# First attention: every third mask of the last two groups made by ScalarE and GpSimd, and the check of counts moved to the GraphSAGE rounds

## The chip, the core and the metric

The kernel runs on one core of a Trainium2 chip. A core has five engines that run their own instruction streams and wait for one another through semaphores: TensorE (PE in the profile, with its weight loads as PEld), VectorE (DVE), ScalarE (ACT), GpSimd (POOL) and SyncE (SP, which only starts transfers here). They share the on-chip memory SBUF; products of TensorE land in the smaller memory PSUM. The metric is the device time of one execution in microseconds (us); lower is better.

## The reference, cut to what matters

A graph of 3,125 nodes with 128 features and 100,000 edges goes through four layers, each with a residual:

```python
h = relu(layernorm(x));  x = x + gat(gat(h))            # two attention layers, 4 heads of 32
h = relu(layernorm(x));  x = x + lanczos(h, edge_weight)  # three products with the weighted graph
h = relu(layernorm(x));  x = x + graphsage(h)             # three rounds: h@Ws + mean over neighbours @Wn, norm, PReLU
h = relu(layernorm(x));  x = x + message_layer(h, edge_type_16)
```

One attention layer, for each head:

```python
e = leaky_relu(al_src[src] + al_dst[dst], 0.2)
w = exp(e - segment_max(e, dst)[dst])
out = segment_sum(h[src] * w / segment_sum(w, dst)[dst], dst) + b ;  x = relu(out)
```

The change touches two places of this: the sums over edges of the first of the two attention layers, and a test that the kernel makes on its own data.

## The kernel before, in words

**The graph as a matrix.** Nodes are laid out in NB = 25 blocks of P = 128. The kernel builds, on the chip, a dense matrix `counts` in 8-bit floats: `counts[source, destination]` is the number of edges between two nodes. It stays in SBUF from the build until the GraphSAGE layer ends. A matrix of summed edge weights goes to DRAM (`weights`) for the second layer.

`place_edges` first scatters the edge records into a table in DRAM, sorted by block of destination and block of source, with 782 indirect transfers that GpSimd issues (L1096). Then `build_block` is called for each of the 25 destination blocks: SyncE loads the slots of the block as soon as the scatters it needs have landed, TensorE transposes them into `keys`, VectorE makes one-hot matrices from the keys (`oh_s`, `oh_d` at L1190, `oh_w` at L1192), TensorE multiplies them into a PSUM bank (L1204, L1207), and ScalarE copies the bank to `counts` (L1211, a cast to 8 bits) and to `w_out` (L1212), whose transfer to DRAM it issues itself (L1215). For the first six blocks ScalarE also copies records into `rowed` (L1177) and keys into `wide_dl` (L1181) for the last layer.

**The check of counts.** The kernel checks that no entry of `counts` exceeds MOST = 15. At the end of each block L1217 runs one activation over the block's column of `counts` (128 x 3200 elements): Relu(counts - 15), written to `junk`, which nobody reads, and summed into one column of `above`. After the last group `above` is summed into a column of `bad` (L1451). `bad` is read by `is_general` (L1955), whose flag decides at the end of the program whether a slow general version has to run; for these inputs it doesn't.

**Attention by thresholds.** exp of a leaky ReLU takes one of two forms, by the sign of its argument, so the sum over edges of one head is split into two matrix products: one with all of `counts` (`u`, L1347), and one with the counts of those pairs whose source score plus destination score is positive. For the second, `attend` makes a mask for each head i and source block sb: a tile `over` of 128 sources by n x 128 destinations (n is the number of destination blocks in the group), bf16, that holds `counts` where `row > minus` and zero elsewhere. `row` is the destinations' scores, which TensorE transposes into PSUM (`ps_row`) once a head; `minus` is one score for each partition. VectorE makes such a mask in one instruction (L1365). TensorE multiplies it with `parts`, the features split in three bf16 terms (L1379), into PSUM tiles `ps_acc`; after the 25 source blocks of a head VectorE sums the three terms (`sums`, L1386), after having made the first two masks of the next head. Masks are made two source blocks ahead of TensorE. At the end of a group some small instructions finish the nodes (L1393 to L1406).

**Groups.** In the first attention the destinations are taken in seven groups: blocks 5 to 8, 9 to 12, 13 to 16, 17 to 20, 21 to 24, then 0 to 2 and 3 to 4. Each group's blocks are built just before it attends, so build and attention interleave. Here VectorE makes every mask: the tuple `pools` has `None` for `beside`, and the pool `stream` of `over` tiles has four buffers.

The second attention works on five groups of five blocks and already shares the masks: `beside` is a pair of pools, `row_of` also copies the row from PSUM into SBUF with ScalarE (L1483), and for every third source block (sb % 3 == 2, eight of 25) ScalarE makes Sign (L1359) and Relu (L1360) of row plus score into `above0` (two buffers), and GpSimd multiplies it by `counts` into `over` of its own pool (three buffers, L1362). Its `stream` has eight buffers. Between the attentions, `project_nodes` (its copies are `gat_xT`, L1268, and `sd`, L1274), `attention_factors` and `source_parts` prepare scores and features.

**The GraphSAGE layer** (`layer2`). For each of five groups of five blocks the input is normalised and `prepare(g, 0)` runs: TensorE transposes the nodes, ScalarE copies them out (`yT`, L1659), TensorE multiplies by the weights into one of two `ps_w` buffers (L1665; in the first round also L1672 for the skips), ScalarE copies `z` (L1667) and half of the skips, VectorE adds `own` (L1668), and `split3` splits z into three bf16 terms with casts on ScalarE and subtractions on GpSimd. Then three rounds: for each of 25 blocks TensorE multiplies `counts` by the terms (`ps_agg`, L1722), VectorE sums and scales; after each group `finish` normalises. After rounds 0 and 1 `prepare` runs for the next one. After round 1 `message_weights` loads the weights of the last layer (its `embT` is cleared at L1768).

**What sets the order.** Each engine runs its instructions in one order, fixed when the program is built. The building framework doesn't keep strictly to the order in which the code issues them: an instruction whose operands and memory are ready may be put ahead of ones that come earlier in the code. Memory is given out from pools that are opened and closed with the blocks of code; a tile in a pool that reuses memory has to wait for the last access to what lay there.

Of the kernel before, what the change touches and what calls it, by code (L numbers as in the profile page):

```python
# [7 lines left out]
F32 = mybir.dt.float32  # L8
BF16 = mybir.dt.bfloat16
I32 = mybir.dt.int32  # L10
U8 = mybir.dt.uint8
FP8 = mybir.dt.float8e4
# [888 lines left out]
class FastGnn(Gnn):  # L901
# [233 lines left out]
    def open_build(self, s, counts):  # L1135
        nc, tc = self.nc, self.tc
        self.counts = counts.tile([P, NB, NP], FP8, name="counts8")
        self.weights = self.dram.tile([NB, P, NP], F32, name="weights")
        self.wide = self.dram.tile([2, sum(N_SLOTS[:WIDE]) * P], BF16, name="wide")
        one = self.b_one = s.enter_context(tc.tile_pool(name="build", bufs=1))  # L1140
        self.b_slots = s.enter_context(tc.tile_pool(name="build_s", bufs=1))
        self.b_hot = s.enter_context(tc.tile_pool(name="build_hot", bufs=2))
        self.b_out = s.enter_context(tc.tile_pool(name="build_out", bufs=3))
        self.b_ps = s.enter_context(tc.tile_pool(name="build_ps", bufs=2, space=PSUM))
        self.b_keys = s.enter_context(tc.tile_pool(name="build_keys", bufs=1, space=PSUM))
        self.lane16 = one.tile([P, P, 2], BF16, name="lane16")
        nc.vector.tensor_copy(self.lane16, bc(self.lane[:, :, None], [P, P, 2]))
        self.minus_most = one.tile([P, 1], F32, name="minus_most")
        nc.vector.memset(self.minus_most, -MOST)
        self.above = one.tile([P, NB], F32, name="above")  # L1150
        self.junk = one.tile([P, NB, P], FP8, name="junk")

    def build_block(self, db):
# [28 lines left out]
        for x0 in range(0, n_slots, BATCH):  # L1182
# [10 lines left out]
            for x in range(k):  # L1193
# [15 lines left out]
                if last and (j == 1 or sb == NB - 1):  # L1209
# [3 lines left out]
                    if sb % 4 == 3 or sb == NB - 1:  # L1213
# [3 lines left out]
        nc.scalar.activation(self.junk, self.counts[:, :, db * P : (db + 1) * P], AF.Relu, bias=self.minus_most,  # L1217
                             accum_out=self.above[:, db : db + 1], saturate=False)
# [115 lines left out]
    def attend(self, suffix, a, b, pools):  # L1334
# [4 lines left out]
        n = b - a  # L1339
        at, cols = slice(a, b), slice(a * P, b * P)  # L1340
# [3 lines left out]
        for q in range(n):  # L1344
            wide = u_tile()
            for sb in range(NB):
                nc.tensor.matmul(wide[:, : HEADS * 3 * F1], lhsT=self.counts[:, sb, (a + q) * P : (a + q + 1) * P],  # L1347
                                 rhs=parts[:, sb, :, :, F1:], start=(sb == 0), stop=(sb == NB - 1))
            V.tensor_reduce(u[:, q], wide[:, : HEADS * 3 * F1].rearrange("p (h s f) -> p h f s", h=HEADS, s=3),
                            axis=AX.X, op=OP.add)  # L1350
        sums = None
        for i in range(HEADS):
            row, own = row_of(lambda j: bc(self.sd[:, a + j, 1, i : i + 1], [P, P]), n)

            def mask(sb, row=row, own=own, i=i):

                if beside and sb % 3 == 2:
                    above = beside[0].tile([P, most * P], BF16, name="above0")[:, : n * P]
                    nc.scalar.activation(above, own, AF.Sign, bias=self.sd[:, sb, 0, i : i + 1])  # L1359
                    nc.scalar.activation(above, above, AF.Relu)  # L1360
                    over = beside[1].tile([P, most * P], BF16, name="over")
# [46 lines left out]
    def graph_and_layer0(self, counts, node):  # L1408
# [3 lines left out]
        with ExitStack() as s:  # L1412
# [17 lines left out]
            with ExitStack() as s2:  # L1430
# [14 lines left out]
                with ExitStack() as s3:  # L1445
                    self.open_build(s3, counts)
                    for a, b in GROUPS:
                        for db in range(a, b):
                            self.build_block(db)
                        self.attend(1, a, b, pools)  # L1450
                    nc.vector.tensor_reduce(self.bad[:, 1:2], self.above, axis=AX.X, op=OP.add)  # L1451
# [175 lines left out]
    def layer2(self):  # L1627
        nc, tc = self.nc, self.tc
        last = 3 * D
        with ExitStack() as s:  # L1630
# [79 lines left out]
            for g in range(GN):  # L1710
# [3 lines left out]
                prepare(g, 0)  # L1714
            for i in range(3):
                n = last + (i == 0)
                ready = []
                for g in range(GN):
                    for db in range(g * GB, (g + 1) * GB):
# [10 lines left out]
                        nc.vector.scalar_tensor_tensor(own[:, db, :], t, inv, own[:, db, :], op0=OP.mult, op1=OP.add)  # L1730
                    finish(g, i)
# [3 lines left out]
                if i == 1:  # L1735
                    self.message_weights(one, ps_msg)
# [298 lines left out]
```

## Time and profile before

| what | value |
|---|---|
| median of 3 runs | 3201.25 us (3200.83 to 3203.47) |
| the profiled execution | 3195.56 us |
| its span | 3193.8 us, 52,069 instructions |
| granted TensorE clock, mean | 0.959 |
| PE busy | 2561.2 us (80%) |
| PEld busy | 1825.5 us (57%) |
| DVE busy | 2296.6 us (72%) |
| ACT busy | 917.4 us (29%) |
| POOL busy | 1445.2 us (45%) |

The stages, by the times at which their instructions run: scatter and build from the start, with the scatter's last issue at about 1,120 us; the first attention interleaved with the build until 1,300 us, its last two groups attending from 1,146 and from 1,258 us; projections until 1,343 us, when the second attention starts; the second layer from about 1,725 to 2,203 us; GraphSAGE from there until about 2,640 us; the message layer to the end.

How to read the lines. In the row of slices each digit is the busy share of an engine in one of 40 equal parts of the span, in tenths, 9 being 90% or more. A row of a group gives line, engine, operation, the tile written, "<-", the tiles read, the shapes (partitions x elements) and xcount, then after the bar the busy time in us and the mean of one in ns, and after the second bar the engine's idle time just before such instructions and who ended it. A row of a timeline gives start and duration in us (a run of equal instructions is joined, with its count), engine, line, operation and tiles, and in brackets the wait before it in us and its releaser. Neighbours overlap by some hundredths of a us to a tenth, so a cost per instruction is best read from start to start.

### The profile page before, as it was taken

How to read it: one execution, taken by the hardware profiler on the slowest of the kernel's cores; microseconds unless marked ns; L12 is line 12 of the kernel's file. 1: busy time of each engine (PE TensorE's matmuls, PEld its weight loads, DVE VectorE, ACT ScalarE, POOL GpSimd, SP SyncE). 2: the span in 40 equal slices, each digit the busy share in tenths (PEclk: the TensorE clock that was granted, in tenths of full speed). 3: DMA queues.
4: the chain of work that ended last, by engine and by line, in shares of the span. 5: the costliest groups of instructions: out<-in, count | busy, mean ns of one | idle time of the engine just before them, and what ended most of it. 6: DMA issues, size and time to landing. Idle time of an engine off the chain costs nothing. (4 is left out here: it accounts for less than half of the span.)

```text
span 3193.8 us, 52069 instructions
## 1 busy us (share of the span) xinstructions
PE 2561.2 (80%) x20788; PEld 1825.5 (57%) x20788; DVE 2296.6 (72%) x4015; ACT 917.4 (29%) x1785; POOL 1445.2 (45%) x1394
## 2 busy tenths in 40 slices
PE   0018787878787788798886999997999976989898
PEld 0017464646455655477675444445555546888897
DVE  7979999999989899899997010405455575666766
ACT  3035050505140212476665000002120212333333
POOL 1577777777777700055553000000120106777775
PEclk9979999999999999899999999998999997999999
DMA  6013130303131101000002878781000004444443
GB/s 187 14 18 98 25 98 20 98 20 101 31 94 28 51 32 62 1 2 1 1 1 80 298 272 302 273 301 45 1 1 1 5 18 138 130 139 133 128 131 85
DMA packets 127742, 276.54 MB, mean 87 GB/s; under 512 B 28645, under 2 KB 68468, under 8 KB 116532
## 3 DMA queue, kind: packets, MB, share of 16 engines
q1 hardware_dynamic: 62982, 198.30, 18.9%
q0 software_dynamic: 37856, 32.76, 4.8%
q10 hardware_dynamic: 26652, 42.05, 3.7%
q8 instruction: 165, 2.70, 0.4%
q14 instruction: 87, 0.71, 0.1%
HBM read 210.00 MB, written 63.02 MB: 85 GB/s over the span
## 5 line engine op out<-in xcount | busy, mean ns | idle before, releaser
L1096 POOL DMA_INDIRECT table<-rec,idx x782 | 773.6, 989 | 336.7 <-issue 237.4
L1365 DVE SCALAR_TENSOR_TENSOR over<-ps_row,minus,counts 128x512 bf16<-128x512 f32 (+3 forms) x1040 | 699.3, 748 | 15.9 <-ACT row L1483 12.0
L1379 PE MATMUL ps_acc<-parts,over 128*128 128x198 bf16 x5000 | 571.4, 251 | 134.1 <-POOL over L1362 34.7
L1379 PEld LDWEIGHTS <-over 128*128 128x128 bf16 x5000 | 391.8, 98 | 309.7 <-DVE over L1365 231.9
L1910 POOL DMA_INDIRECT m_far<-pre,src x401 | 397.8, 992 | 259.1 <-DVE skips L923 137.2
L1207 PE MATMUL ps_cw<-oh_w,oh_d 128*128 128x128 bf16 x4050 | 385.9, 224 | 56.7 <-DVE oh_w L1192 52.1
L1533 PE MATMUL ps_sum<-g,node 128*128 128x512 f32 (+1 forms) x1050 | 413.2, 552 | 12.9 <-DMA g<-weights 12.9
L1362 POOL TENSOR_TENSOR over<-above,counts 128x640 bf16<-128x640 bf16 x160 | 211.3, 1329 | 392.0 <-ACT above L1360 265.2
L1207 PEld LDWEIGHTS <-oh_d 128*128 128x128 bf16 x4050 | 303.8, 100 | 90.9 <-issue 68.7
L1204 PE MATMUL ps_cw<-oh_d,oh_s 128*128 128x128 bf16 x1350 | 299.0, 224 | 48.2 <-ACT w_out L1212 24.7
L1722 PE MATMUL ps_agg<-l_parts,counts 128*128 128x384 bf16 (+1 forms) x1875 | 317.3, 327 | 14.0 <-POOL l_parts L923 14.0
L1192 DVE TENSOR_TENSOR oh_w<-oh_s,keys 128x1024 bf16<-128x1024 bf16 (+2 forms) x561 | 325.4, 633 | 0.0
L1533 PEld LDWEIGHTS ps_sum<-g,node 128*128 128x128 f32 x1050 | 189.8, 192 | 222.1 <-issue 208.4
L1722 PEld LDWEIGHTS <-counts 128*128 128x128 fp8e4 x1875 | 183.5, 98 | 134.5 <-issue 11.3
L1754 POOL IOTA of_i<- 96x1 int32 x1 | 0.1, 135 | 480.2 <-PE ps_sum L1609 480.2
L1211 ACT ACTIVATE counts<-ps_cw 128x256 fp8e4<-128x256 f32 (+1 forms) x325 | 122.7, 378 | 303.9 <-PE ps_cw L1207 294.4
L1931 PE MATMUL agg_far<-m_far,oh_far 128*128 128x128 f32 x1246 | 173.8, 287 | 11.6 <-ACT m_far L1917 7.1
L1892 PE MATMUL agg_wide<-m_wide,oh_wide 128*128 128x128 f32 x1100 | 160.3, 289 | 26.5 <-ACT m_wide L1889 17.9
L1204 PEld LDWEIGHTS <-oh_s 128*128 128x128 bf16 x1350 | 133.6, 100 | 80.9 <-issue 49.9
L1347 PEld LDWEIGHTS <-counts 128*128 128x128 fp8e4 x1250 | 112.1, 98 | 102.3 <-ACT counts L1211 19.9
L1885 PE MATMUL ps_m<-skips,src_hot 128*128 128x128 bf16 x1650 | 159.3, 224 | 9.1 <-DVE src_hot L1875 9.1
L1931 PEld LDWEIGHTS agg_far<-m_far,oh_far 128*128 128x128 f32 x1246 | 156.6, 199 | 13.6 <-ACT m_far L1917 9.0
(353 smaller groups left out, 3532.1 us busy)
## 6 DMA issues: line engine op xcount, KB each, us to landing
g<-weights SPq DMA_DIRECT2D x75, 1024.0 KB
g<-weights SPq DMA_DIRECT2D x75, 576.0 KB
weights<-w_out ACTq DMA_DIRECT2D x150, 256.0 KB
src_row<-wide SPq DMA_DIRECT2D x32, 512.0 KB
table<-rec,idx POOLq DMA_INDIRECT x782
type_row<-wide SPq DMA_DIRECT2D x32, 384.0 KB
table<-none SPq DMA_DIRECT2D x1, 10864.0 KB
type_row<-types SPq DMA_DIRECT2D x25, 384.0 KB
```

The source lines that it names most:

```text
L1096: st = nc.gpsimd.indirect_dma_start(out=self.table, out_offset=bass.IndirectOffsetOnAxis(ap=idx[k][:, p : p + 1], axis=0), in_=rec[:, (k * ...
L1192: nc.vector.tensor_tensor(oh_w[:, t, :h], oh_s[:, :h], key(WT + t), op=OP.mult)
L1204: nc.tensor.matmul(ps[:, 0, j, :], lhsT=oh_s[of], rhs=oh_d[of], start=(j == c == 0), stop=last, skip_group_check=True)
L1207: nc.tensor.matmul(ps[:, 1, j, :], lhsT=oh_d[of], rhs=oh_w[:, t][of], start=False, stop=(last and t == 2), skip_group_check=True)
L1362: nc.gpsimd.tensor_tensor(over[:, : n * P], above, self.counts[:, sb, cols], op=OP.mult)
L1365: V.scalar_tensor_tensor(over[:, : n * P], row, minus[:, sb, i : i + 1], self.counts[:, sb, cols], op0=OP.is_gt, op1=OP.mult)
L1379: nc.tensor.matmul(banks[j // 2][:, j % 2, : 3 * F2], lhsT=over[:, j * P : (j + 1) * P], rhs=parts[:, sb, i].rearrange("p s f -> p (s f)") ...
L1533: nc.tensor.matmul(ps[:, c0 // 512, :m], lhsT=node[:, b, :], rhs=g[:, c0 - lo : c0 - lo + m], start=(b == 0), stop=(b == NB - 1))
L1722: nc.tensor.matmul(ps[:, :n], lhsT=self.counts[:, sb, db * P : (db + 1) * P], rhs=parts[:, sb, :n], start=(sb == 0), stop=(sb == NB - 1))
L1892: nc.tensor.matmul(agg, lhsT=oh[:, j, :], rhs=m[:, j, :], start=(x == 0), stop=(x == n_slots - 1))
L1910: nc.gpsimd.indirect_dma_start(out=m[:, j, :], out_offset=None, in_=pre, in_offset=bass.IndirectOffsetOnAxis(ap=src_of[:, a + j : a + j + ...
L1931: nc.tensor.matmul(agg[d], lhsT=oh[:, c - lo, :], rhs=m[:, c - a, :], start=(c == LOW[d]), stop=(c == ENDS[d] - 1))
```

## The change

Three things:

1. The tiles `minus_most`, `above` and `junk` leave the build's pool, and with them the memset, the 25 checks at the ends of the blocks, and the reduction after the last group.
2. In the first attention, groups 0 to 2 and 3 to 4 (`b <= FIRST`, FIRST = 5) use `shared` instead of `pools`: the row is also copied into SBUF by ScalarE (`two_rows`), and every third mask goes over ScalarE and GpSimd as in the second attention, with tiles 3 x 128 columns wide, two `above0` and three `over` buffers. `stream` keeps its four. The other five groups are as before. (`wide` is renamed `ps` where it named a PSUM tile.)
3. In `layer2`, before the rounds, the three tiles and the memset appear, and after the sums of a block in groups 1, 2 and 3 one check is issued as long as any is left: 15 in round 0 and ten in round 1. After round 1, before `message_weights`, `above` is summed into `bad`.

```diff
@@ -1145,10 +1145,6 @@
         self.b_keys = s.enter_context(tc.tile_pool(name="build_keys", bufs=1, space=PSUM))
         self.lane16 = one.tile([P, P, 2], BF16, name="lane16")
         nc.vector.tensor_copy(self.lane16, bc(self.lane[:, :, None], [P, P, 2]))
-        self.minus_most = one.tile([P, 1], F32, name="minus_most")
-        nc.vector.memset(self.minus_most, -MOST)
-        self.above = one.tile([P, NB], F32, name="above")
-        self.junk = one.tile([P, NB, P], FP8, name="junk")
 
     def build_block(self, db):
         nc, tc = self.nc, self.tc
@@ -1214,8 +1210,6 @@
                         b = sb // 4 * 4
                         nc.scalar.dma_start(self.weights[db, :, b * P : (sb + 1) * P].rearrange("p (b s) -> p b s", s=P),
                                             w_out[:, : sb + 1 - b])
-        nc.scalar.activation(self.junk, self.counts[:, :, db * P : (db + 1) * P], AF.Relu, bias=self.minus_most,
-                             accum_out=self.above[:, db : db + 1], saturate=False)
 
     def load_graph(self, dst, b, weights=False):
         self.nc.sync.dma_start(dst.rearrange("p b s -> p (b s)"), self.weights[b])
@@ -1337,16 +1331,17 @@
         V = nc.vector
         stream, done, u_tile, acc_tile, row_of, most, beside = pools
         n = b - a
+        wide = GW if most == GB else 3 * P
         at, cols = slice(a, b), slice(a * P, b * P)
         parts, minus = self.parts, self.gat_small[3]
         u = done.tile([P, most, HEADS, F1], F32, name="u")[:, :n]
         acc = done.tile([P, most, HEADS, F2], F32, name="acc")[:, :n]
         for q in range(n):
-            wide = u_tile()
+            ps = u_tile()
             for sb in range(NB):
-                nc.tensor.matmul(wide[:, : HEADS * 3 * F1], lhsT=self.counts[:, sb, (a + q) * P : (a + q + 1) * P],
+                nc.tensor.matmul(ps[:, : HEADS * 3 * F1], lhsT=self.counts[:, sb, (a + q) * P : (a + q + 1) * P],
                                  rhs=parts[:, sb, :, :, F1:], start=(sb == 0), stop=(sb == NB - 1))
-            V.tensor_reduce(u[:, q], wide[:, : HEADS * 3 * F1].rearrange("p (h s f) -> p h f s", h=HEADS, s=3),
+            V.tensor_reduce(u[:, q], ps[:, : HEADS * 3 * F1].rearrange("p (h s f) -> p h f s", h=HEADS, s=3),
                             axis=AX.X, op=OP.add)
         sums = None
         for i in range(HEADS):
@@ -1355,10 +1350,10 @@
             def mask(sb, row=row, own=own, i=i):
 
                 if beside and sb % 3 == 2:
-                    above = beside[0].tile([P, most * P], BF16, name="above0")[:, : n * P]
+                    above = beside[0].tile([P, wide], BF16, name="above0")[:, : n * P]
                     nc.scalar.activation(above, own, AF.Sign, bias=self.sd[:, sb, 0, i : i + 1])
                     nc.scalar.activation(above, above, AF.Relu)
-                    over = beside[1].tile([P, most * P], BF16, name="over")
+                    over = beside[1].tile([P, wide], BF16, name="over")
                     nc.gpsimd.tensor_tensor(over[:, : n * P], above, self.counts[:, sb, cols], op=OP.mult)
                 else:
                     over = stream.tile([P, most * P], BF16, name="over")
@@ -1444,11 +1439,21 @@
                          lambda: ps_acc.tile([P, 2, 256], F32, name="ps_acc"), row_of, 4, None)
                 with ExitStack() as s3:
                     self.open_build(s3, counts)
+                    rows = s3.enter_context(tc.tile_pool(name="gat_d", bufs=1))
+                    beside = [s3.enter_context(tc.tile_pool(name=f"gat_b{n}", bufs=n)) for n in (2, 3)]
+
+                    def two_rows(term, n):
+                        own = rows.tile([P, 3 * P], F32, name="row")[:, : n * P]
+                        whole, _ = row_of(term, n)
+                        nc.scalar.copy(own, whole)
+                        return whole, own
+
+
+                    shared = pools[:4] + (two_rows, 4, beside)
                     for a, b in GROUPS:
                         for db in range(a, b):
                             self.build_block(db)
-                        self.attend(1, a, b, pools)
-                    nc.vector.tensor_reduce(self.bad[:, 1:2], self.above, axis=AX.X, op=OP.add)
+                        self.attend(1, a, b, shared if b <= FIRST else pools)
                 with ExitStack() as s3:
                     tmp = s3.enter_context(tc.tile_pool(name="gat_h", bufs=1))
                     two = s3.enter_context(tc.tile_pool(name="gat_r", bufs=2))
@@ -1712,6 +1717,12 @@
                 self.normal(tmp, y[:, at], self.x[:, at], GB)
                 nc.vector.tensor_scalar(y[:, at], y[:, at], 0.0, None, op0=OP.max)
                 prepare(g, 0)
+
+            minus_most = one.tile([P, 1], F32, name="minus_most")
+            nc.vector.memset(minus_most, -MOST)
+            above = one.tile([P, NB], F32, name="above")
+            junk = one.tile([P, NB, P], FP8, name="junk")
+            unseen = list(range(NB))
             for i in range(3):
                 n = last + (i == 0)
                 ready = []
@@ -1728,11 +1739,16 @@
                         t = tmp.tile([P, D], F32, name="agg_t")
                         nc.vector.tensor_reduce(t, ps[:, :last].rearrange("p (s f) -> p f s", s=3), axis=AX.X, op=OP.add)
                         nc.vector.scalar_tensor_tensor(own[:, db, :], t, inv, own[:, db, :], op0=OP.mult, op1=OP.add)
+                        if unseen and 0 < g < GN - 1:
+                            b = unseen.pop()
+                            nc.scalar.activation(junk, self.counts[:, :, b * P : (b + 1) * P], AF.Relu, bias=minus_most,
+                                                 accum_out=above[:, b : b + 1], saturate=False)
                     finish(g, i)
                 if i < 2:
                     for g in range(GN):
                         prepare(g, i + 1)
                 if i == 1:
+                    nc.vector.tensor_reduce(self.bad[:, 1:2], above, axis=AX.X, op=OP.add)
                     self.message_weights(one, ps_msg)
```

## The prediction

> **What bounds the kernel now.** I read the page's slices first, then groups by line and shape, then timelines of single engines. The page's chain of waits covers only 46% of the span, roughly from 1,700 us on (its pieces after 2,203 us are used below), so the first attention is read from groups and timelines. The slices:
>
> ```profile
> DVE  7979999999989899899997010405455575666766
> ACT  3035050505140212476665000002120212333333
> POOL 1577777777777700055553000000120106777775
> ```
>
> A slice is 80 us. VectorE (DVE) is full in slices 3 to 16, build and both attentions. GpSimd (POOL) is idle in slices 14 to 16, where the last two groups attend (from 1,146 and 1,258 us), and ScalarE (ACT) is nearly idle there. The groups by shape between 1,100 and 1,330 us, and VectorE's timeline:
>
> ```profile
> L1365 DVE SCALAR_TENSOR_TENSOR over<-ps_row,minus,counts 128x384 bf16<-128x384 f32 x100 | 53.0, 622 | 0.0
> L1365 DVE SCALAR_TENSOR_TENSOR over<-ps_row,minus,counts 128x256 bf16<-128x256 f32 x100 | 39.6, 474 | 0.0
> ...
> 1161.61 13.22 DVE L1365 SCALAR_TENSOR_TENSOR over<-ps_row,minus,counts 128x384 bf16<-128x384 f32 x25
> 1174.73 0.84 DVE L1386 TENSOR_REDUCE acc<-ps_acc 128x132 f32<-128x396 f32 x2
> ...
> 1270.68 9.88 DVE L1365 SCALAR_TENSOR_TENSOR over<-ps_row,minus,counts 128x256 bf16<-128x256 f32 x25
> ```
>
> One head of group (0,3) is 25 masks and two sums, 13.87 us from 1,161.61 to the next head's 1,175.48; of (3,5), 10.27 us. VectorE never waits in them: it sets their time. A mask costs 0.53 us start to start at 384 columns and 0.39 at 256.
>
> **The change, part by part.** The sum is made against the profiled execution: 3,195.56 us, of which 3,193.8 are span. The shown median is 5.69 us above it, so I take the same difference off the median.
>
> *1. The check leaves the build.* 25 activations over 128x3200 go. ScalarE's timeline at one of them, and who waits:
>
> ```profile
> 1112.26 2.97 ACT L1217 ACTIVATE junk<-counts,minus_most 128x3200 fp8e4<-128x3200 fp8e4 x1
> ...
> 1115.22 0.22 ACT L1181 COPY wide_dl<-keys 128x76 bf16<-128x76 bf16 x1
> ...
> 1115.47 0.69 DVE L1190 TENSOR_TENSOR oh_s<-lane,keys 128x1024 bf16<-128x1024 bf16 x1 [2.24 <-ACT wide_dl L1181]
> ```
>
> A check holds ScalarE 2.96 us (1,112.26 to 1,115.22). Behind it waits the copy of keys, and for that VectorE: 2.26, 2.24 and 1.88 us at blocks 1, 2 and 4, together 6.4, which go. In the one-slot blocks 20 to 23 TensorE waits for ScalarE's `w_out` after a check (1.01, 1.60 and 1.42 us) and is the later engine until the block ends, so VectorE's waits there shrink by about 4. Elsewhere VectorE covers the check and nothing is won. Value **-10**; ends -6 (only the direct waits) and -14 (also the 2.09 us at 1,126.62, where TensorE runs slow after standing idle).
>
> *2. Every third mask on ScalarE and GpSimd.* VectorE makes 17 of 25: a head needs 17 x 0.525 + 0.75 = 9.7 us at 384 columns and 17 x 0.392 + 0.48 = 7.1 at 256. The eight others each take Sign and Relu on ScalarE and one multiplication on GpSimd. None is in the trace at these widths; the nearest rows are the second attention's, at 640:
>
> ```profile
> L1362 POOL TENSOR_TENSOR over<-above,counts 128x640 bf16<-128x640 bf16 x160 | 211.3, 1329 | 392.0 <-ACT above L1360 265.2 <-PE ps_acc L1379 123.5 <-POOL over L1362 1.9
> ...
> 1439.87 10.38 DVE L1365 SCALAR_TENSOR_TENSOR over<-ps_row,minus,counts 128x640 bf16<-128x640 f32 x13
> ```
>
> GpSimd at 384: 0.80 us if all of 1,325 ns scales, 0.83 if 0.1 us is fixed as in its smallest fill (98 ns); I take 0.80, and 0.55 at 256. ScalarE's steps fall by 0.83 ns an element, 0.21 us per operation at 384 and 0.32 at 256. The trace shows two rhythms at 640. With two `above0` buffers ScalarE often waits for GpSimd: two masks then cost 4.23 us (1,439.06 to 1,443.29). In the other rhythm a mask costs 1.59 us (1,355.69 to 1,357.28). The first becomes 4.23 - 2 x 0.50 - 0.43 = 2.8 a pair, 11.2 a head, at 384, and 2.1 and 8.3 at 256; the second 1.16 a mask, 9.8 with the row copy, and 8.0. The second attention's inner heads average 14.9 us (row copies at 1,435.97 and 1,480.66, three heads), near VectorE's own 17 x 0.79 + 1.24 = 14.7, so I stay near the faster rhythm: 10.5 and 8.2. That saves 4 x (13.87 - 10.5) + 4 x (10.27 - 8.2) = 13.5 + 8.3 = 21.8. Off it: filling and draining the chain at each group's ends, and ScalarE's copy of the next block's `rowed`, queued among the signs and waiting for its load (2.86 us in ScalarE's timeline at 1,153.80). Value **-19**. Ends: -12 (slow rhythm throughout), -27 (VectorE alone binds).
>
> A rule speaks against this part. The Trainium skill (SBUF — State Buffer, section SBUF: two separate sides) says that GpSimd holds a port pair for a whole instruction, and that a VectorE operation with two SBUF inputs stands still meanwhile. The row first: the 13 masks above took 0.798 us each beside a working GpSimd, against 0.79 from the shape alone. A mask has one tensor in SBUF (`counts`) and its row in PSUM. By the rule's lock eight multiplications would hold VectorE 8 x 0.80 = 6.4 us a head, more than the 4.2 it saves: part 2 would cost some 9 us in (0,3). The lock is real in this trace, where both inputs are in SBUF (0.35 us becomes 1.63 beside a GpSimd addition):
>
> ```profile
> 2281.76 2.18 POOL L1704 TENSOR_TENSOR skips<-skips,l_own 128x640 f32<-128x640 f32 x1 [24.94 <-DVE inv_col L1727]
> ...
> 2282.46 1.63 DVE L1730 SCALAR_TENSOR_TENSOR l_own<-agg_t,inv_col,l_own 128x128 f32<-128x128 f32 x1
> ```
>
> For masks I go by their row. Dispatch of the scatter is over by then (POOL has no instruction after 1,120 us), so GpSimd's queue is empty.
>
> *3. The build's memory frees earlier.* ScalarE's `gat_xT` waits 37.0 us for the reduction of `above` at L1451. With `above` gone that memory ends with block 4 at 1,258 us, and groups 1 to 4 of the second projection can start under group (3,5); their copies into `sd` still wait for the last signs, which read it. Group 0 needs the attention's result at 1,305.8. Value **-2**, ends 0 and -4.
>
> *4. The check enters the GraphSAGE stage.* By its place in the code a check follows a block's aggregation in groups 1 to 3 of rounds 0 and 1. There ScalarE idles 18.3 us between normalisations and TensorE's 97 us of products cover 15 checks (44 us). But an engine's order is made by readiness, not by place. VectorE's timeline has
>
> ```profile
> 2205.52 0.14 DVE L1768 MEMSET embT<- 32x96 f32 x1
> ```
>
> which stands behind round 1 in the code and runs 280 us before that. A check needs only `counts` and a bias memset like this one. So I expect checks as soon as layer 2's memory exists (2,203.4 us), in each pause of ScalarE. The preparation from 2,205.7 to 2,256.9 us has such pauses and no cover: TensorE starts its 97 us only when it ends. ScalarE's timeline for one group:
>
> ```profile
> 2233.36 0.37 ACT L1667 COPY z<-ps_w 128x256 f32<-128x256 f32 x1
> 2233.62 0.38 ACT L484 COPY skips<-ps_w 128x256 f32<-128x256 f32 x1
> 2236.16 0.37 ACT L1667 COPY z<-ps_w 128x256 f32<-128x256 f32 x1 [2.16 <-PE ps_w L1665]
> 2237.03 0.37 ACT L484 COPY skips<-ps_w 128x256 f32<-128x256 f32 x1 [0.49 <-PE ps_w L1672]
> 2237.79 0.27 ACT L1667 COPY z<-ps_w 128x128 f32<-128x128 f32 x1 [0.38 <-PE ps_w L1665]
> ...
> 2240.91 0.36 ACT L1667 COPY z<-ps_w 128x256 f32<-128x256 f32 x1
> ```
>
> A group takes 7.55 us (2,233.36 to 2,240.91) and calls ScalarE in about three visits, one per turn of the two `ps_w` buffers, with 3.5 us of copies and casts. A check in the pause before each visit makes it 3 x 2.96 + 3.5 = 12.4 us, +4.85. Behind a check wait z, then TensorE for the buffer, then GpSimd's `l_parts`, then the first sums. Four groups: +19.4; the first, which starts amid the normalisations and takes six checks, +5.5 by the same steps. Together **+25** for some 18 checks; the other seven fall under round 0 at no cost. Ends: 0 (all in the rounds), and +49.5 if the preparation takes all 25: 25 x 2.96 = 74, less the 24.5 us of pauses in that timeline. The moved final reduction (0.17 us) is nothing.
>
> Sum: -10 - 19 - 2 + 25 = **-6**: 3,189.6 for the profiled execution, **3,195 us** against the median.
>
> **The rivals.**
> *The checks stay in the rounds.* Part 4 is 0: -31, 3,170 us. For it: ScalarE's free 18.3 us, and that a placement could be kept. Against: embT, and the sum over `bad` for the end of the program, which runs at 1,316.85.
> *Slower: the preparation takes all 25 checks.* Place: ScalarE's queue, 2,205 to 2,257 us. If z and skip of one turn are called on separate visits, there are more than 25 pauses (the timeline has 28), and part 4 costs 49.5: -31 + 49.5 = +18.5, 3,220 us. It decides from 31 us on, about 21 checks at 1.5 net. Against: after a stop of 2.96 us both buffers are ready together.
> *Third masks come late.* TensorE takes masks in order and VectorE has four buffers here, eight in the second attention. If every pair stops VectorE, (0,3) gives 4 x 1.5 and (3,5) nothing, so part 2 is -4 with its losses: +9, 3,210 us. For it: the 34.7 us that TensorE waits for GpSimd's masks in the second attention; against: its inner heads of 14.9.
>
> **Chances.** Main case 0.50, own range 3,184 to 3,206; checks in the rounds 0.17; all checks in the preparation 0.18; late masks 0.15. A change under 0.2% (6.4 us) counts as none here. The main case lies near that bound: 0.26 faster, 0.22 same, 0.02 slower. Rival one is all faster; two is slower (0.16) or same (0.02); three 0.02, 0.05 and 0.08. Faster 0.45, same 0.29, slower 0.26. The range leaves out the lower half of rival one and most of rival two's upper half: 3,168 to 3,218.
>
> **What would show it.** L1365's 384 and 256 shapes fall to 68 each, with heads of 10.5 and 8.2 us between row copies. No wait for `wide_dl` at blocks 1, 2 and 4. The start of TensorE's long run of `ps_agg` comes about 51 us after layer 2's first square now; after, 76, with checks between z copies. The prediction is wrong if checks stand in the rounds, if masks make VectorE wait, or if ScalarE loads tables between Sign and the copies into `counts`.

## The result and the profile after

The changed kernel takes **3207.03 us** (median; 3203.33 to 3213.55) against 3201.25 us before: ratio **1.0018** (95% interval 1.0012 to 1.0024), 5.8 us slower. The prediction said 3,195 us, 6 us faster. The time lies inside the stated range, but the kernel became slower where it was to become faster.

The profiled execution of the changed kernel took 3210.43 us (span 3208.5), that of before 3195.56. Of the 14.9 us between them some 9 are a difference of executions: the one before is 5.7 us under its median, the one after 3.4 over. So I compare stages, between marks that both traces have; "(0, 3)" is the group of destination blocks 0 to 2.

| stretch, us | before | after | difference |
|---|---|---|---|
| start to the end of group (17, 21) | 865.5 | 866.5 | +1.0 |
| to the end of group (21, 25) | 131.7 | 127.2 | -4.5 |
| to the first mask of (0, 3) | 149.0 | 150.2 | +1.2 |
| to the end of (0, 3) | 64.8 | 50.7 | -14.1 |
| to the first mask of (3, 5) | 47.3 | 44.9 | -2.4 |
| to the end of (3, 5) | 46.5 | 41.6 | -4.9 |
| to the second attention | 40.0 | 35.8 | -4.2 |
| **sum up to the second attention** | 1344.9 | 1317.0 | **-27.9** |
| second layer's last product to TensorE's long run of `ps_agg` | 53.8 | 86.6 | **+32.8** |

An "end" here is the start of the addition of the bias to that group (L1405 before, L1400 after). The "preparation" below is the last row: the stretch of the GraphSAGE layer from the second layer's last product until TensorE runs `ps_agg` without a break. The second attention takes 388.6 us in both, from its first mask to its last addition of the bias; the second layer's products, which nothing touches, took 428.2 us in the execution of before and 433.4 in that of after, and 431 to 435 in the kernels of the first experiments. In the slices, ScalarE fills up where the GraphSAGE layer starts (slice 27), and GpSimd and ScalarE work in slices 14 and 15:

```profile
DVE  7979999999989898999993010413455575566766
ACT  3043040404121155766662000007420212233333
POOL 1577777777777732455551000001120106777775
```

VectorE's timeline in the last two groups, (0, 3) and then (3, 5), after the change:

```profile
1157.84 9.00 DVE L1360 SCALAR_TENSOR_TENSOR over<-ps_row,minus,counts 128x384 bf16<-128x384 f32 x17
1166.76 0.83 DVE L1381 TENSOR_REDUCE acc<-ps_acc 128x132 f32<-128x396 f32 x2
1167.51 9.01 DVE L1360 SCALAR_TENSOR_TENSOR over<-ps_row,minus,counts 128x384 bf16<-128x384 f32 x17
...
1263.11 6.74 DVE L1360 SCALAR_TENSOR_TENSOR over<-ps_row,minus,counts 128x256 bf16<-128x256 f32 x17
1269.77 0.56 DVE L1381 TENSOR_REDUCE acc<-ps_acc 128x132 f32<-128x396 f32 x1
1270.25 5.96 DVE L1360 SCALAR_TENSOR_TENSOR over<-ps_row,minus,counts 128x256 bf16<-128x256 f32 x15
```

A head is 17 masks and the sums, 9.67 us (1157.84 to 1167.51) and 7.14 us (1263.11 to 1270.25), with no wait: VectorE's own time, the best end of what the prediction allowed. GpSimd's multiplications beside it, by shape:

```profile
L1357 POOL TENSOR_TENSOR over<-above,counts 128x384 bf16<-128x384 bf16 x32 | 27.7, 868 | 34.7 <-PE ps_acc L1374 21.5 <-ACT above L1355 5.9 <-ACT counts L1207 5.0
L1357 POOL TENSOR_TENSOR over<-above,counts 128x256 bf16<-128x256 bf16 x32 | 20.3, 640 | 71.9 <-ACT counts L1207 45.7 <-PE ps_acc L1374 20.3 <-ACT above L1355 5.1
```

GpSimd needs 868 and 640 ns (800 and 550 were estimated). Eight of them a head are 6.9 us of GpSimd's time, and VectorE's masks beside them stay at 0.53 us: no lock held them. The rule that the prediction set against this part is, in its own words, one of two inputs in SBUF; a mask has one there (`counts`) and its row in PSUM, so the rule did not reach it.

ScalarE's timeline in the preparation, for about one group:

```profile
2214.51 3.02 ACT L1744 ACTIVATE junk<-counts,minus_most 128x3200 fp8e4<-128x3200 fp8e4 x1
...
2217.85 0.37 ACT L1672 COPY z<-ps_w 128x256 f32<-128x256 f32 x1 [0.23 <-PE ps_w L1670]
2219.07 0.37 ACT L484 COPY skips<-ps_w 128x256 f32<-128x256 f32 x1 [0.85 <-PE ps_w L1677]
2219.34 2.96 ACT L1744 ACTIVATE junk<-counts,minus_most 128x3200 fp8e4<-128x3200 fp8e4 x1
...
2223.23 0.77 ACT L1664 COPY yT<-ps_t 128x512 f32<-128x512 f32 x2
2223.86 3.00 ACT L1744 ACTIVATE junk<-counts,minus_most 128x3200 fp8e4<-128x3200 fp8e4 x1
2226.82 0.75 ACT L922 CAST l_parts<-rest 128x640 bf16<-128x640 f32 x1
2227.44 0.40 ACT L1672 COPY z<-ps_w 128x256 f32<-128x256 f32 x1
```

The checks stand there, between the copies of z. The first begins at 2,184.98 us, and 21 of the 25 start before TensorE's long run does. ScalarE is busy for 81.4 of the 86.6 us, against 24.0 of 53.7 without checks.

### The profile page after: what moved, and what is told of

Its sections match the earlier page's. It is cut to its first block, busy times and chain, and to the rows that moved or that the text cites. A ratio compares the mean times of both kernels' runs of the same rounds, so it can differ in the third digit from the quotient of the medians.

```text
span 3208.5 us, 52208 instructions
## 1 busy us (share of the span) xinstructions
PE 2552.6 (80%) x20788; PEld 1840.4 (57%) x20788; DVE 2267.3 (71%) x3951; ACT 977.3 (30%) x1921; POOL 1495.7 (47%) x1458
## 5 line engine op out<-in xcount | busy, mean ns | idle before, releaser
L1360 DVE SCALAR_TENSOR_TENSOR over<-ps_row,minus,counts 128x512 bf16<-128x512 f32 (+3 forms) x976 | 670.0, 759 | 16.5 <-ACT row L1488 12.0
L1374 PE MATMUL ps_acc<-parts,over 128*128 128x198 bf16 x5000 | 549.7, 251 | 123.7 <-POOL over L1357 34.8
L1357 POOL TENSOR_TENSOR over<-above,counts 128x640 bf16<-128x640 bf16 (+2 forms) x224 | 259.3, 1165 | 314.4 <-PE ps_acc L1374 165.2
L1354 ACT ACTIVATE above<-row,sd 128x640 bf16<-128x640 f32 (+2 forms) x224 | 166.7, 747 | 60.7 <-POOL over L1357 57.6
L1200 PEld LDWEIGHTS <-oh_s 128*128 128x128 bf16 x1350 | 133.7, 100 | 71.0 <-issue 50.5
```

Source lines behind the costliest of these rows:

```text
L1200: nc.tensor.matmul(ps[:, 0, j, :], lhsT=oh_s[of], rhs=oh_d[of], start=(j == c == 0), stop=last, skip_group_check=True)
L1357: nc.gpsimd.tensor_tensor(over[:, : n * P], above, self.counts[:, sb, cols], op=OP.mult)
L1360: V.scalar_tensor_tensor(over[:, : n * P], row, minus[:, sb, i : i + 1], self.counts[:, sb, cols], op0=OP.is_gt, op1=OP.mult)
L1374: nc.tensor.matmul(banks[j // 2][:, j % 2, : 3 * F2], lhsT=over[:, j * P : (j + 1) * P], rhs=parts[:, sb, i].rearrange("p s f -> p (s f)") ...
```

## The experiments

The expectations name theories by letters. **A**: the loss is the price of the checks in the preparation, and only there. **R**: leaving the build gained little because the check had stood in a wait of ScalarE. **G**: early signs of the shared masks wait for GpSimd's scatter. **P** and **S** are two ways of pricing a check in a pause. The rivals are in the expectations. Where nothing else is said, the edits are made to the changed kernel.

Four of these kernels (`twelve`, `short`, `anch_rowed` and `anch_both`) ran on another chip, where the kernel before takes 4366.94 us and the second attention starts some 940 us later (why that chip is slower is not known). I use them by stages, and their ratios only against that chip's own time before.

### Checks held in the rounds

```diff
-            minus_most = one.tile([P, 1], F32, name="minus_most")
-            nc.vector.memset(minus_most, -MOST)
+            minus_most = one.tile([P, NB], F32, name="minus_most")
...
                             b = unseen.pop()
-                            nc.scalar.activation(junk, self.counts[:, :, b * P : (b + 1) * P], AF.Relu, bias=minus_most,
-                                                 accum_out=above[:, b : b + 1], saturate=False)
+                            nc.vector.tensor_scalar(minus_most[:, b : b + 1], t[:, :1], 0.0, -MOST, op0=OP.mult, op1=OP.add)
+                            nc.scalar.activation(junk, self.counts[:, :, b * P : (b + 1) * P], AF.Relu,
+                                                 bias=minus_most[:, b : b + 1], accum_out=above[:, b : b + 1], saturate=False)
```

> The changed kernel, but each check takes its bias (-15) from a column that VectorE writes out of the sums of the block just aggregated, so it cannot run before that block's products. Theory A (the checks cost what they cost only because they stand in the preparation, where ScalarE has no cover): the trace shows 15 checks in round 0 and 10 in round 1, the preparation is back at about 53 us, and the kernel is 28 us faster than before (the changed kernel's own gain up to the second attention), ratio 0.991. Theory B (a check costs wherever it stands in this layer, because the squares and PReLU steps of the next group wait behind it): each of 25 checks still costs about 1.3 us, the rounds grow by 33 us, ratio about 1.002 as for the changed kernel.

Measured: 3174.81 us, ratio **0.9909** (0.9893 to 0.9924). The groups by tile (duration least/median/most in ns, then first and last start) and TensorE's timeline of this kernel:

```profile
L1744 ACT ACTIVATE junk<-counts,minus_most x25: 2963/2964/2966, 2257.5 to 2422.8; 128x3200 fp8e4<-128x3200 fp8e4 x25
```

```profile
2237.53 97.33 PE L1732 MATMUL ps_agg<-l_parts,counts 128*128 128x385 bf16 x587 [1.70 <-POOL l_parts L923]
```

All 25 checks run, each as long as before, and start between 2,257 and 2,423 us, beside TensorE's products; the preparation is 53.7 us and the rounds did not grow (363.6 us from the long run's start to the last product of `ps_agg`, 364.0 before). The same 25 instructions cost 33 us in one place and nothing in the other: theory A.

### No check, neither change, and the move alone

`no_check` drops the check from `layer2` (and with it the tiles and the memset):

```diff
-                        if unseen and 0 < g < GN - 1:
-                            b = unseen.pop()
-                            nc.scalar.activation(junk, self.counts[:, :, b * P : (b + 1) * P], AF.Relu, bias=minus_most,
-                                                 accum_out=above[:, b : b + 1], saturate=False)
...
-                    nc.vector.tensor_reduce(self.bad[:, 1:2], above, axis=AX.X, op=OP.add)
```

`bare` has this edit and the next one, which drops the sharing; `moved_only` has the next one alone:

```diff
-                        self.attend(1, a, b, shared if b <= FIRST else pools)
+                        self.attend(1, a, b, pools)
```

> The changed kernel with the check of counts left out altogether (no entry of counts is tested). Theory A: build, masks and projections together gain 28 us and nothing else moves, ratio 0.991; it equals the anchored kernel within 3 us. Theory B (the 33 us longer preparation has another cause than the checks, such as layer 2's loads or a slower clock of TensorE): the preparation stays above 75 us and the ratio near 1.00.

> The check left out altogether and no shared masks (all masks of the first attention on VectorE): what leaving the build is worth by itself. By the windows of the changed kernel's trace the build gains 5 us and the projections 4: -9 us, ratio 0.997. By the prediction's own steps it is -12 (10 and 2), ratio 0.996. If the check was fully covered in the build, it is -4 at most.

> The check moved as in the changed kernel, without the shared masks. Theory A: -9 (build and projections) and +33 (21 checks in the preparation): +24 us, ratio 1.0075, and checks stand between copies of z as in the changed kernel. With the prediction's sizes (-12 and +25) it is +13, ratio 1.004. The masks' own worth is the changed kernel less this one: -19 expected.

| kernel | median, us | ratio (95%) | second attention starts | preparation |
|---|---|---|---|---|
| before | 3203.05 | 1 | 1344.9 | 53.8 |
| `bare` | 3199.79 | 0.9990 (0.9983 to 0.9997) | 1341.7 | 53.8 |
| `no_check` | 3177.78 | 0.9920 (0.9907 to 0.9934) | 1320.1 | 53.7 |
| `anchored` | 3174.81 | 0.9909 (0.9893 to 0.9924) | 1319.8 | 53.7 |
| `moved_only` | 3236.44 | 1.0102 (1.0086 to 1.0117) | 1344.9 | 86.8 |

The preparation is 86.6 to 86.8 us with the moved checks and 53.7 to 53.8 without: **+33.0**. The masks are worth the difference of pairs: 22.0 us (`bare` less `no_check`) and 27.6 (`moved_only` less the changed kernel, each taken against the time before that was measured beside it). By stages it is 16.8 in (0, 3) (67.5 us in `bare`, 50.7 in `no_check`) and 8.5 in (3, 5) (50.5 and 42.0), so about **-25**. Leaving the build, with the memory that it frees, is worth **3 us**, where the prediction had said 12. `no_check` came as theory A said. `bare` missed its expectation of -9, and with it `moved_only` its +24 (+33 was measured): the -9 was made from windows of the trace after in which masks and build overlap.

### Why leaving the build gained so little

ScalarE's timeline from the end of block 0's build into block 1's, before:

```profile
1069.51 2.97 ACT L1217 ACTIVATE junk<-counts,minus_most 128x3200 fp8e4<-128x3200 fp8e4 x1
...
1072.46 0.24 ACT L1181 COPY wide_dl<-keys 128x100 bf16<-128x100 bf16 x1
1078.35 0.73 ACT L1177 COPY rowed<-slots 76x128 bf16<-76x128 bf16 x2 [5.65 <-DMA slots<-table]
```

and in `bare`, with VectorE's wait after it:

```profile
1065.44 0.26 ACT L1177 COPY wide_dl<-keys 128x100 bf16<-128x100 bf16 x1
...
1074.28 0.72 ACT L1173 COPY rowed<-slots 76x128 bf16<-76x128 bf16 x2 [8.58 <-DMA slots<-table]
...
1079.44 0.69 DVE L1186 TENSOR_TENSOR oh_s<-lane,keys 128x1024 bf16<-128x1024 bf16 x1 [3.95 <-PE ps_cw L1200]
```

Without the check `wide_dl` comes 2.9 us sooner, and then ScalarE waits 2.93 us longer (8.58 for 5.65) for the load of the next block's slots, in front of the copy into `rowed`. Both times `rowed` starts 9.2 us after the last copy of counts began. The copies of counts of the block under way are queued behind it, TensorE waits for their banks, and VectorE, which is now ahead, waits for TensorE: 3.95 us, in place of 2.26 for `wide_dl`. The test is to take that copy from ScalarE, in the kernel before (`before_rowed`, check in the build) and in `bare` (`bare_rowed`, no check):

```diff
-                    nc.scalar.copy(rowed[:rows, i], r[:rows, :, f])
-                    nc.scalar.dma_start(self.wide[i, (at + a * rows) * P : (at + (a + 1) * rows) * P].rearrange(
+                    nc.vector.tensor_copy(rowed[:rows, i], r[:rows, :, f])
+                    nc.sync.dma_start(self.wide[i, (at + a * rows) * P : (at + (a + 1) * rows) * P].rearrange(
```

> The kernel before (check in the build, no shared masks) with the copies into rowed on VectorE and their transfers issued by SyncE. Theory R (in the build the check stands in time that ScalarE would spend waiting for the load of slots in front of the copy into rowed, so leaving the build gains nothing there): with that wait gone VectorE's 2.09 us wait at block 2 and some shorter ones go, 2 to 5 us faster than before, ratio 0.999, and the check is now worth more (see the next kernel). Theory Q (the check is covered by other work, not by that wait): this kernel and the next differ by 3 us, as the kernel before and the bare one do.

> The same, and the check left out altogether (no entry of counts is tested; no shared masks). Theory R: 8 us faster than the bare kernel by the waits for ps_cw at blocks 1 and 2 that go (3.95 and 3.99 us), ratio 0.9965, and 6 to 9 us faster than the kernel with the check above. Theory Q: 3 us faster than it.

Measured: `before_rowed` 3204.05 us, 1.0007 (0.9999 to 1.0016); `bare_rowed` 3190.61 us, **0.9967** (0.9957 to 0.9978). With `rowed` off ScalarE the checks in the build cost 13.4 us (6 to 9 were expected), with it on ScalarE 3.3. `before_rowed` alone did not gain its 2 to 5 us: with the check in its place VectorE still waits 2.26, 2.24 and 1.87 us for `wide_dl`. Each of the two stops hid the other. In `bare_rowed` VectorE's waits of 3.95 and 3.99 us for TensorE's banks are gone.

A second loss stands in every kernel whose check has left the build, and this edit does not touch it. `ps_u`, the PSUM tile of the products `u`, has one buffer. VectorE's timeline around block 2's build, before:

```profile
1112.66 0.57 DVE L1349 TENSOR_REDUCE u<-ps_u 128x132 f32<-128x396 f32 x1 [2.03 <-PE ps_u L1347]
...
1146.22 2.19 DVE L1365 SCALAR_TENSOR_TENSOR over<-ps_row,minus,counts 128x384 bf16<-128x384 f32 x4
1148.31 0.57 DVE L1349 TENSOR_REDUCE u<-ps_u 128x132 f32<-128x396 f32 x1
```

and in `bare`, with TensorE's last products `u` of the group:

```profile
1142.62 0.58 DVE L1344 TENSOR_REDUCE u<-ps_u 128x132 f32<-128x396 f32 x1
1143.10 2.21 DVE L1360 SCALAR_TENSOR_TENSOR over<-ps_row,minus,counts 128x384 bf16<-128x384 f32 x4
1147.91 0.57 DVE L1344 TENSOR_REDUCE u<-ps_u 128x132 f32<-128x396 f32 x1 [2.60 <-PE ps_u L1342]
...
1143.30 4.57 PE L1342 MATMUL ps_u<-parts,counts 128*128 128x396 bf16 x25
```

Before, VectorE empties `ps_u` at 1,112.66 us, while it has to wait for `wide_dl` anyway, and TensorE spreads the next 25 products among those of the build. In `bare` that reduction stands behind all one-hot matrices of block 2, so the 25 products start only at 1,143.30 us, behind the build, and the attention waits for them. From the first to the fifth mask it takes 5.29 us in place of 2.57, and in (3, 5) 5.89 in place of 2.83: 5.8 us in all. This is read from the traces; no run gave `ps_u` a second buffer.

The edit to `rowed` on top of the anchored kernel, first on the other chip (`anch_both` has the second edit below too):

> The anchored kernel, with the copies of records into rowed made by VectorE and their transfers issued by SyncE, so that ScalarE never waits for the load of slots. Theory R (without the check ScalarE runs straight into the copy of rowed, which waits for the load of slots, and TensorE's banks and then VectorE wait behind it, some 4 us at blocks 1 and 2): those waits of VectorE for ps_cw go, the copies add 14 x 0.15 = 2 us, and it is 5 us faster than the anchored kernel (0.991 to 0.9895). Theory Q (the same wait appears elsewhere, because TensorE's transposes need the same load and VectorE needs them): 0 to +3 us against the anchored kernel.

```diff
-            nc.scalar.copy(self.wide_dl[:, at : at + n_slots], keys[:, DL, :n_slots])
+            nc.vector.tensor_copy(self.wide_dl[:, at : at + n_slots], keys[:, DL, :n_slots])
```

> As the kernel before it, and the copy of keys into wide_dl by VectorE too. Theory R: VectorE's two waits for wide_dl (1.9 and 1.7 us) go as well, 8 us faster than the anchored kernel (ratio 0.9885). Theory Q: the wait for the last counts copies of a block is then VectorE's for a PSUM bank, and nothing comes beyond the kernel with rowed alone.

Measured there: 4329.42 us, 0.9921 (0.9901 to 0.9941), and 4328.88 us, 0.9919 (0.9903 to 0.9935). The stretch from the fifth group's end to the end of (0, 3) is 192.7 and 192.1 us, against 200.0 and 199.8 in `twelve` and `short`, which have the copy on ScalarE: 7 us, where R said 5. `wide_dl` on VectorE adds nothing, where R said 3 more. Then beside the anchored kernel on a chip like the first:

> The anchored kernel a second time, beside the next one on the same chip: 28 us faster than before, ratio 0.991 on a chip where before takes 3,203 us.

> The anchored kernel with the copies into rowed on VectorE and their transfers on SyncE a second time, on the same chip as the anchored one: 7 to 8 us faster than it by theory R (the stretch from the fifth group's end to the sixth's was 192.7 us against about 200 on the other chip), ratio 0.9885; 0 if the other chip's slow start made the difference.

Measured: 3176.41 us, 0.9932 (0.9918 to 0.9945), and 3174.76 us, 0.9919 (0.9905 to 0.9932). The 7 us did not come here. The timelines of VectorE, ScalarE and GpSimd in the second of these kernels (the sign is L1354):

```profile
1129.43 0.69 DVE L1186 TENSOR_TENSOR oh_s<-lane,keys 128x1024 bf16<-128x1024 bf16 x1 [9.02 <-PE ps_cw L1200]
...
1122.74 0.61 ACT L1354 ACTIVATE above<-row,sd 128x384 bf16<-128x384 f32 x1 [9.65 <-POOL over L1357]
...
1120.84 0.97 POOL L1096 DMA_INDIRECT table<-rec,idx  x1 [0.30 <-issue]
1121.83 0.88 POOL L1357 TENSOR_TENSOR over<-above,counts 128x384 bf16<-128x384 bf16 x1
```

GpSimd issues the scatter until 1,121.8 us. A sign for a shared mask, placed ahead of the copies of counts in ScalarE's queue, needs a buffer that GpSimd frees only after that. On the other chip the scatter had ended (last issue at 1,180 us) long before this block was built (2,050 us). The test holds the signs back until the group's last block has its counts:

```diff
+        score = self.sd[:, :, 0]
+        if beside and suffix == 1:
+            score, top = self.gat_small[:2]
+            V.tensor_scalar(top[:, 0, :1], self.counts[:, NB - 1, b * P - 1 : b * P], 0.0, None, op0=OP.mult)
+            V.tensor_scalar(score, self.sd[:, :, 0], top[:, 0, :1], None, op0=OP.add)
...
-                    nc.scalar.activation(above, own, AF.Sign, bias=self.sd[:, sb, 0, i : i + 1])
+                    nc.scalar.activation(above, own, AF.Sign, bias=score[:, sb, i : i + 1])
```

> The anchored kernel with the copies into rowed on VectorE and their transfers on SyncE, and the signs of the first attention held back: their bias is a copy of the scores that VectorE makes only when the last block of the group has its counts, so no sign stands in ScalarE's queue during the group's build. Theory G (on this chip GpSimd still issues the scatter until 1,121 us; the signs placed early in ScalarE's queue wait for it, 9.65 us before the sign at 1,122.74, and the copies of counts, TensorE's banks and VectorE wait behind: 9.02 us at 1,129.43): that wait goes, some 2 us of masks made early are lost, and it is 5 to 7 us faster than without the holding (3,174.8 against 3,168 to 3,170, ratio 0.990). Theory N (the wait is another's): the ratio stays at 0.992 and VectorE still waits some 9 us in block 2.

> The anchored kernel with the signs held back as above, the copies into rowed on ScalarE as in the changed kernel. Theory G with theory R: ScalarE's wait for the load of slots ends at about the same time as GpSimd's scatter, so taking only one of the two away gains nothing: within 3 us of the anchored kernel (ratio 0.992). If the two waits add up, it is 5 us faster.

Measured: `held_rowed` **3168.68 us, 0.9899** (0.9884 to 0.9914); `held_only` 3177.00 us, 0.9919 (0.9906 to 0.9933). Both as theory G said. VectorE's waits for TensorE's banks at blocks 1 and 2 are 3.83 and 4.14 us in `held_only`, one of 9.02 with `rowed` alone moved, and none in `held_rowed`: only both stops removed bring the 6 to 8 us. `held_rowed` starts the second attention at 1,312.4 us and is the fastest of all, with every check in place.

### What a check costs in a pause

`twelve`:

```diff
-            unseen = list(range(NB))
+            nc.vector.memset(above, 0.0)
+            unseen = list(range(12))
```

> The changed kernel with checks for 12 of the 25 blocks only (13 blocks of counts are not tested). All 12 should run in the preparation, from its start on. Theory P (a price for each check: 33 us over 21 checks, 1.57 each, because each lands in one of ScalarE's short pauses and overhangs it): +19 us against no check at all, preparation 54 + 19 = 73 us, ratio 0.992 + 0.006 = 0.998. Theory S (the pauses are a pool that the checks fill first: 12 x 2.96 less the 24.5 us of pauses): +11, preparation 65 us, ratio 0.9955.

`short`:

```diff
-                            nc.scalar.activation(junk, self.counts[:, :, b * P : (b + 1) * P], AF.Relu, bias=minus_most,
+                            nc.scalar.activation(junk[:, :12], self.counts[:, :12, b * P : (b + 1) * P], AF.Relu, bias=minus_most,
```

> The changed kernel with each of the 25 checks over 12 of the 25 source blocks only (128x1536; the other 13 source blocks of each column are not tested). By the shape a check takes about 1.5 us. Theory P (in proportion): half the price for about the same 21 to 25 checks, +16 to 20 us, preparation 70 to 73. Theory S (ScalarE becomes full only where checks and copies together exceed the time; a check that is no longer than a pause is free): 25 x 1.5 = 37 less most of the 24.5 us of pauses, +13 or less, preparation 67 or less, ratio 0.996. In both, nothing but the preparation differs from the anchored kernel.

Measured: `twelve` 4358.10 us, 0.9979 (0.9966 to 0.9992); `short` 4342.73 us, 0.9942 (0.9924 to 0.9961). Without checks in it the preparation is the same to 0.2 us on both chips, so its length decides:

| kernel | checks in it, length of one | preparation, us | price of one, us |
|---|---|---|---|
| no check | 0 | 53.8 | |
| `twelve` | 12 x 3.00 | 75.1 | 21.3 / 12 = 1.78 |
| after | 21 x 2.99 | 86.6 | 32.8 / 21 = 1.56 |
| `short` | 23 x 1.58 | 65.1 | 11.3 / 23 = 0.49 |

Each theory is half right. Each of twelve checks costs at least as much as each of 21, as P said: they do not first fill a pool of 24.5 us of pauses. But at half the length a check costs a third, and the preparation stays under S's 67 us. Both results fit a price of what overhangs the check's own pause, here the length less 1.1 to 1.4 us; only these three kernels suggest it.

## Why the prediction was wrong

Its sum was -10 - 19 - 2 + 25 = -6. The runs have about -3 for the build and the memory together (9 us less gain than said), -25 for the masks (6 us more) and +33 for the moved checks (8 us dearer): +5, against +5.8 measured. Two steps failed, parts 1 and 4; part 2 erred the other way and hid 6 of their 17 us, which is luck.

- **Part 4** missed by 8 us, and the mechanism was right: the order of an engine is made by readiness, the checks rise into the preparation, stretch each group there and hold TensorE back. A group takes 13.4 us in the trace after (12.4 worked out, 7.55 before). The size failed in the count ("some 18 checks", and 21 stand there) and in the price (1.39 us a check, and it was 1.56). 21 checks was named as the point from which the slower rival decides, and so it was, at 33 us and not its 49.5. The start of TensorE's long run comes 81 us after layer 2's first square; 76 was announced.
- **Part 1** is the step that failed in kind. It took VectorE's waits for `wide_dl` and TensorE's for `w_out` as the check's price, and did not ask what stood next in ScalarE's queue, nor what VectorE did in those waits. In the one-slot blocks the 4 us came (-4.5 in the stretch to the fifth group's end, after +1.0 before it). At blocks 1 and 2 the copy into `rowed` waits for the load of slots until the same moment with or without the check, and the late reduction of `ps_u` takes 5.8 us at the start of the last two groups. "No wait for `wide_dl` at blocks 1, 2 and 4" is false for two of the three: 1.90 and 1.71 us are left, since the copy stands behind the last copies of counts. With part 3 in it this -12 was -3; even part 1's milder bound of -6 was too much. (Its other bound adds up wrongly: 6.4 + 4 + 2.09 is 12.5, not 14.)
- **Part 2** gained more than said: -25 for -19. Its better bound ("VectorE alone binds") holds for (0, 3): 9.67 us a head, not 10.5. In (3, 5) the later heads reach 7.14 and the first two don't, where VectorE waits for TensorE.
- **Part 3** has the 2 us and more behind the attention: in `bare`, which has no shared masks, that stretch is 4.2 us shorter (40.0 to 35.8 us), and 30 matmuls of the second projection's L1266 run inside (3, 5), where 20 did. But (3, 5) itself is 4.0 us longer there (46.5 to 50.5), 3.1 of it between the first and the fifth mask, where the products `u` are late and no matmul of the projection runs yet. Of the other 0.9 us, 0.57 is a wait of VectorE for TensorE's `ps_acc`; whether the projection's matmuls cause it is open.

The rival of late masks did not come: VectorE's masks have no idle time before them in (0, 3), and 3.1 us in all in (3, 5), 2.7 of it for TensorE's `ps_acc`. The rival in which checks stay in the rounds is what `anchored` makes true, at -28 us where the prediction said -31.

## What to carry to other kernels

A piece of work that only fills time has to be tied to the work that is to cover it, by a value it reads; where it stands in the code is not a place. When a wait is taken off an engine, read what is next in that engine's queue and when its own input arrives: a stop in front of a later arrival is free, and two stops that end at about the same time show nothing until both are gone. Ask also what else ran in that wait: work that it let through early may now come late. Price an intruder by what overhangs the pause it falls into, times the number of pauses, not by the sum of idle time.

## What the runs showed that was not expected

- The 25 checks of 2.96 us cost 3 us or 13 in the build, by who copies 14 small pieces of records.
- Masks shared with an engine that looked idle in the slices are made ready early, while it is still busy: the multiplication that frees their buffer starts at 1,121.83 us, behind the scatter, and that put 9.02 us on VectorE.
- After the longer preparation the first round runs slower: 99.01 us for TensorE's run of 585 products against 97.33 for 587. The granted clock over the run's first 16 us is 0.87 (1.00 before), and 0.82 in the preparation (0.87 before).
- A wait can do useful work for another engine: VectorE emptied `ps_u` in the wait that the check caused, and without that wait the next products `u` came 2.7 and 3.1 us later.
